# Convolved attention scores from convolved keys and shifted unconvolved values, with the values projected pixel-major for all heads and kept in DRAM

## The chip, the cores and the metric

The kernel runs on one core of a Trainium2 chip. The metric is the device time of one execution in microseconds, as the median of several executions. All data are 32-bit floats. The engines are named as the profile names them: PE (matrix multiply; PEld are its weight loads), DVE (vector), ACT (scalar), POOL (GpSimd) and SP, which here only issues transfers (DMAs).

## The reference

Two layers are applied to a batch of 4 images with 512 channels and 64 × 64 pixels. Layer 0 is a linear attention over two sets of 64 heads; layer 1 is a set of edge filters. The change lies in layer 0.

```
q, k, v = h @ wq.T, h @ wk.T, h @ wv.T                    # 1x1 projections, 512 -> 512 each
qkv = concat([q, k, v])                                   # 1536 channels = 64 heads x (8 q, 8 k, 8 v)
dw  = conv5x5_depthwise(qkv)                              # SAME padding, one 5x5 kernel per channel
pw  = conv1x1_grouped(dw)                                 # groups of 8 channels
f   = concat([qkv, pw]).reshape(B, 128 heads, 24, 4096)   # 64 plain heads, 64 convolved heads
query, key, value = relu(f[:, :, :8]), relu(f[:, :, 8:16]), f[:, :, 16:]
value_pad = concat([value, ones])                         # 9 rows
scores = einsum('bhdn,bhen->bhde', value_pad, key)        # 9 x 8 per head, summed over the 4096 pixels
out = einsum('bhde,bhen->bhdn', scores, query)
out = out[:, :, :8] / (out[:, :, 8:] + 1e-15)
y = conv1x1(out, proj_kernel) * inv + shift + x           # 1024 -> 512 channels
# layer 1: Sobel, Laplace, diagonal and gradient maps of y, four 512 -> 128 branches with GELU,
# an attention over channels, a 512 -> 512 fuse, a norm over channels, GELU, + y
```

For a convolved head the score of value row d and key row e is a sum over pixels of (convolved value d) × (convolved key e). The convolution of the value is linear: it is a weighted sum over 25 shifts and 8 channels of the plain value.

## The kernel before

**Layout.** The heads are cut into four groups of 16 (`Group`, `g` = 0 to 3), so one group has 128 channels each of keys, values and queries, one channel per partition. An image is cut into eight strips of 512 pixels: `STRIPS` names them by half (rows 0 to 31, 32 to 63) and by `k`; strip `k` holds the rows `k`, `k + 4`, ... of its half. There are 16 groups of work in all (4 images × 4).

**A group's work.** `project` (L199) multiplies a strip of x by a 128-column weight matrix (four matmuls of 128 × 512 into one PSUM bank), ACT copies it to `strip`, and four DMAs write it into `inps[t]`, a padded image in the layout that the convolution needs. `turn` (L232) transposes keys and values to pixel-major tiles on PE, and `scores` (L245) forms the plain scores from them. `convolve` (L318) does the 5 × 5 and 1 × 1 convolution of one half of the image for keys, values or queries: 10 shifts × 16 matmuls on 32 × 32 tiles of the PE array, with weights `mat` that POOL builds. `conv_turn` (L349) transposes convolved keys and values, `conv_scores` (L361) makes their scores: each matmul gives 32 × 32 products, of which only the 8 × 8 blocks of equal heads are kept, by a mask in `conv_sums` (L378). `conv_fold` (L406) multiplies the convolved scores into the projection, `conv_denominators` and `conv_divide` (L417, L426) make the convolved heads, and `denominators` and `divide` the plain ones. Results go to DRAM (`heads`, `cheads`, `folded`).

**The order of the work.** PE's instructions stand in the order in which the program writes them; the order on the other engines and on SP is made by the framework from priorities and buffers. `keys_and_values` writes out the first part of a group (16 projections, seven `turn`, six `scores`, with the query convolution of the group before between them), `queries` the second (eight projections, the last `turn` and two `scores`, four convolutions of keys and values, their turns and scores). After each step `run` calls `advance`, which lets a share of the later stages of the image before run on PE: `project_out` (the 1024 → 512 projection), `edge_branches` (filters and branches) and `fuse_out`. The share is in proportion to a cost that is written beside each step (`T_PROJ` = 3.4, `T_CONV` = 8.6 and so on). So image 0 has no other stage beside it, images 1 to 3 have the later stages of the image before between their steps, and the later stages of image 3 stand alone at the end.

**Buffers.** x strips pass through `xst` (five tiles of 128 × 1024), weights through `gw`, most intermediate tiles through `work` (22 tiles of 128 × 512). All DMAs are issued by SP, on one queue, in order. In PSUM four banks hold single tiles (`ps_tile`) and four hold the quads of `convolve` and of the divisions (`quad_tiles`).

Of the kernel before, what the change touches and what calls it, by code (L numbers as in the profile page):

```python
# [15 lines left out]
P = 128  # L16
# [21 lines left out]

NB = H // 4 + 1
STRIPS = [(half, k) for half in range(2) for k in range(4)]  # L40
DXS = (0, -2, -1, 1, 2)

# [3 lines left out]
for _name, _n in (("ident", P), ("bdmask", P), ("hmask", 32), ("spread", P), ("csum", P), ("mmask", 4), ("jmask", 4)):  # L46
    CONST[_name] = slice(_at, _at + _n)
    _at += _n
# [8 lines left out]
T_PROJ, T_TURN, T_SCORES, T_CONV, T_SMALL = 3.4, 0.9, 0.3, 8.6, 0.9  # L57
# [8 lines left out]
def conv_seq_kernel(  # L66
    ctx: ExitStack, tc, x, wqkv, dpk, proj, projc, bn0, consts, vec, watt1, batt1, watt2, wbr, wfuse, out
# [11 lines left out]
    gw = front.enter_context(tc.tile_pool(name="gw", bufs=3))  # L79
    work = front.enter_context(tc.tile_pool(name="work", bufs=22))  # L80
# [8 lines left out]
    def quad_tiles(name):  # L89
        return [psum.tile([P, 512], F32, tag="quad", name=name) for _ in range(4)]  # L90

# [24 lines left out]
    for t in (KEY, VALUE, QUERY):  # L116
        inps[t] = keep.tile([P, 4, NB, W], F32, name=f"inp{t}")
        nc.gpsimd.memset(inps[t][:, :, 0, :], 0.0)
        nc.gpsimd.memset(inps[t][:, :, NB - 1, :], 0.0)

    vts = []
    for n in range(3):
        vt = keep.tile([P, 4, 4, 33], F32, name=f"vt{n}")
        nc.gpsimd.memset(vt, 1.0)
        vts.append(vt)

# [47 lines left out]
    class Group:  # L174


        def __init__(self, b, heads, cheads, folded, g):
            self.b, self.heads, self.cheads, self.folded, self.g = b, heads, cheads, folded, g
            self.w, self.mat, self.xs = {}, {}, {}
            self.strip, self.rq, self.held, self.conv = {}, {}, {}, {}  # L180
# [3 lines left out]
        def load_w(self, t):  # L184
            self.w[t] = gw.tile([P, NCH, P], F32, name="w_sb", tag="w_sb")
            nc.sync.dma_start(out=self.w[t], in_=wqkv[self.g, t])

        def load_mat(self, t):

            dp = gw.tile([P, 4, 48], F32, name="dp_sb", tag="dp_sb", bufs=2)  # L190
            nc.sync.dma_start(out=dp, in_=dpk[self.g, t])
# [15 lines left out]
        def project(self, t, j):  # L207
            half, k = STRIPS[j]
            if t != VALUE and j not in self.xs:
                self.load_x(j)  # L210
            ps = ps_tile("proj")
# [4 lines left out]
            if t != KEY:  # L216
                del self.xs[j]
            s = work_tile("strip")
            nc.scalar.copy(s, ps)  # L219
            self.strip[t, j] = s  # L220
# [4 lines left out]
            if t == QUERY:  # L225
                rq = work_tile("rq")
                nc.gpsimd.tensor_scalar(rq, self.strip.pop((t, j)), 0.0, None, ALU.max)  # L227
                self.rq[j] = rq
# [4 lines left out]
        def turn(self, j):  # L233
            kt_ps, vt_ps = ps_tile("tr"), ps_tile("tr")
            for n in range(4):
                nc.tensor.transpose(kt_ps[:, ts(n, P)], self.strip[KEY, j][:, ts(n, P)], ident)
            kt = work_tile("kt")
            nc.scalar.activation(kt, kt_ps, AF.Relu)
            for n in range(4):
                nc.tensor.transpose(vt_ps[:, ts(n, P)], self.strip[VALUE, j][:, ts(n, P)], ident)  # L240
            vt = vts[j % 3]
            nc.vector.tensor_copy(
                vt.rearrange("p n q d -> p (n q) d")[:, :, 0:32], vt_ps.rearrange("p (a d) -> p a d", d=32)
            )
            self.held[j] = kt, vt  # L245
            del self.strip[KEY, j], self.strip[VALUE, j]

        def scores(self, j):
            kt, vt = self.held.pop(j)
            ps = ps_tile("s")  # L250
            for n in range(4):
                for q in range(4):
                    nc.tensor.matmul(  # L253
                        ps[32 * q : 32 * q + 32, 0:33], lhsT=kt[:, P * n + 32 * q : P * n + 32 * q + 32],
                        rhs=vt[:, n, q, :], start=(n == 0), stop=(n == 3),
                    )
            if j == 0:
                self.s = small.tile([P, 33], F32, name="s_sb")
# [3 lines left out]
            if j == NJ - 1:  # L262
                self.ks = small.tile([P, 32], F32, name="ks_sb")
                nc.vector.tensor_scalar(self.ks, hmask, self.s[:, 32:33], None, ALU.mult)
                self.sb = small.tile([P, 4, 32], F32, name="sbd", bufs=1)
# [5 lines left out]
        def fold_turn(self):  # L271
# [3 lines left out]
            self.st = small.tile([P, P], F32, name="stt", bufs=1)  # L275
# [44 lines left out]
        def convolve(self, t, half):  # L320
# [14 lines left out]
            for i in range(4):  # L335
                o = work_tile("co")
                if t == KEY:
                    if half == 0 and i == 0:
                        self.ksum = small.tile([P, 2, 4], F32, name="ksum")
                    nc.scalar.activation(o, banks[i], AF.Relu, accum_out=self.ksum[:, half, i : i + 1])  # L340
# [558 lines left out]
```

## Time and profile before

| quantity | value |
|---|---|
| median of 3 runs | 5212.99 us (5206.63 to 5223.82) |
| the profiled execution's own time | 5216.06 us |
| its span in the profile | 5214.3 us |
| image 0, no later stage beside it | 0 to about 800 us |
| images 1 to 3 with the later stages of the image before | about 800 to 4433 us |
| the later stages of image 3 | 4433 to 5214 us |

In the profile a group line gives the source line, the engine, the operation, output <- input, the shapes and the count, then the busy time in us, the mean ns of one, and the idle time of the engine before it with what ended it. A 32-bit matmul is recorded as two passes, so 1,536 projections' matmuls are 3,072 records. Matmuls are pipelined: what a block of them takes is read from the distance of the starts in the timeline, not from the duration of one.

### The profile page before, as it was taken

Reading aid. Unit: us, or ns where it says so; the run is one execution under the profiler, and the core shown is the slowest. Engines: PE = TensorE matmul, PEld = TensorE weight load, DVE = VectorE, ACT = ScalarE, POOL = GpSimd, SP = SyncE. Lnnn points to the kernel's source line nnn. Section 1 sums busy time; section 2 is a strip of 40 time slices with the busy share of each in tenths; the row PEclk is TensorE's granted clock in tenths of the full one; section 3 lists DMA queues with packets and bytes.
Section 4 is the critical chain, followed back from the end, with each engine's and each line's share of the span. In section 5 each row is a group of like instructions: output and inputs, shape, how many; then the busy total and the mean of one; then the engine's idle time right before and its main releaser. Section 6 shows DMA issues by size and latency. Waiting matters only on the chain. (4 is left out here: it accounts for less than half of the span.)

```text
span 5214.3 us, 116246 instructions
## 1 busy us (share of the span) xinstructions
PE 4864.4 (93%) x50514; PEld 2567.1 (49%) x50514; DVE 2185.7 (42%) x3084; ACT 1616.6 (31%) x2569; POOL 638.1 (12%) x435
## 2 busy tenths in 40 slices
PE   8999999998999999999999999999989999899777
PEld 3544444444555554444455555444445555445443
DVE  1222222113555643421355645342124655446975
ACT  1111111001444533300134443331013544225765
POOL 1010110000101012300010000240000101000335
PEclk9999999999999999999999999999999999899989
DMA  5445455664544544576545454657654544575435
GB/s 180 145 159 158 150 180 174 154 149 120 174 153 154 172 152 158 182 203 151 151 143 175 138 176 140 187 171 205 149 144 151 182 143 150 151 185 143 147 116 167
DMA packets 534095, 832.18 MB, mean 160 GB/s; under 512 B 192464, under 2 KB 264656, under 8 KB 531536
## 3 DMA queue, kind: packets, MB, share of 16 engines
q1 hardware_dynamic: 533584, 824.74, 53.7%
q8 instruction: 397, 6.50, 0.5%
q14 instruction: 114, 0.93, 0.1%
HBM read 546.09 MB, written 177.75 MB: 139 GB/s over the span
## 5 line engine op out<-in xcount | busy, mean ns | idle before, releaser
L213 PE MATMUL proj<-xt,w_sb 128*128 128x512 f32 x3072 | 1426.2, 609 | 85.7 <-DMA xt<-in_x 51.9
L328 PE MATMUL cv<-inp,mat 32*32 32x504 f32 (+2 forms) x30720 | 1061.9, 594 | 25.6 <-issue 20.3
L213 PEld LDWEIGHTS proj<-xt,w_sb 128*128 128x128 f32 x3072 | 572.2, 194 | 778.2 <-issue 640.0
L528 PE MATMUL yps<-hd,fold_sb 128*128 128x512 f32 x2048 | 897.2, 595 | 15.5 <-DMA hd<-heads 15.4
L328 PEld LDWEIGHTS cv<-inp,mat 32*32 32x32 f32 x30720 | 627.0, 103 | 440.8 <-issue 214.7
L528 PEld LDWEIGHTS yps<-hd,fold_sb 128*128 128x128 f32 x2048 | 386.5, 190 | 508.2 <-issue 475.7
L219 ACT COPY strip<-proj 128x512 f32<-128x512 f32 x384 | 223.6, 583 | 1299.8 <-PE proj L213 1263.4
L603 PE MATMUL br<-maps,wbr_sb 128*128 128x256 f32 x2048 | 484.1, 389 | 40.5 <-ACT maps L586 25.3
L533 DVE SCALAR_TENSOR_TENSOR yt<-yps,shift,xr 128x512 f32<-128x512 f32 x128 | 96.0, 750 | 935.9 <-PE yps L528 880.0
L681 PE MATMUL zps<-ef,wf_sb 128*128 128x512 f32 x1024 | 461.5, 602 | 18.4 <-DVE z L685 8.7
L603 PEld LDWEIGHTS br<-maps,wbr_sb 128*128 128x128 f32 x2048 | 392.1, 194 | 161.8 <-issue 58.9
L227 POOL TENSOR_SCALAR rq<-strip 128x512 f32<-128x512 f32 x128 | 213.2, 1666 | 1789.9 <-ACT strip L219 1167.2
L193 POOL TENSOR_TENSOR mat<-dp_sb 128x1280 f32<-128x1280 f32 x48 | 117.7, 2453 | 1786.6 <-PE cv L328 1136.9
L681 PEld LDWEIGHTS zps<-ef,wf_sb 128*128 128x128 f32 x1024 | 195.8, 193 | 264.4 <-issue 233.0
L576 DVE TENSOR_TENSOR maps<-dv 128x1054 f32<-128x1054 f32 x128 | 164.0, 1281 | 349.4 <-PE br L603 349.4
L610 ACT ACTIVATE ef_o<-br,shift,scale 128x256 f32<-128x256 f32 x256 | 142.4, 560 | 374.1 <-PE br L603 362.3
L292 DVE RECIPROCAL rec<-rec 128x512 f32<-128x512 f32 x64 | 214.4, 3351 | 1.6
L688 POOL TENSOR_TENSOR total<-total,sq 128x512 f32<-128x512 f32 x96 | 129.8, 1352 | 681.2 <-ACT sq L683 667.3
L685 DVE TENSOR_SCALAR z<-zps,fbias 128x512 f32<-128x512 f32 x128 | 95.0, 744 | 260.2 <-DMA out<-z 90.0
L706 POOL TENSOR_TENSOR z<-z,yr 128x512 f32<-128x512 f32 x128 | 174.3, 1379 | 227.4 <-ACT z L703 125.0
L582 ACT ACTIVATE lap<-maps 128x524 f32<-128x524 f32 x128 | 81.6, 638 | 315.8 <-DVE maps L580 311.5
L261 DVE TENSOR_TENSOR s_sb<-s_sb,s 128x33 f32<-128x33 f32 x112 | 20.8, 186 | 370.2 <-PE s L253 370.2
(121 smaller groups left out, 4131.0 us busy)
## 6 DMA issues: line engine op xcount, KB each, us to landing
xt<-in_x SPq DMA_DIRECT2D x512, 512.0 KB, 4.9
inp<-strip SPq DMA_DIRECT2D x1536, 64.0 KB, 2.7
win<-y SPq DMA_DIRECT2D x128, 396.0 KB, 4.3
y<-yt SPq DMA_DIRECT2D x128, 264.0 KB, 4.8
yr<-y SPq DMA_DIRECT2D x128, 264.0 KB, 3.4
xr<-in_x SPq DMA_DIRECT2D x128, 256.0 KB, 5.8
heads<-q SPq DMA_DIRECT2D x128, 256.0 KB, 3.1
hd<-heads SPq DMA_DIRECT2D x128, 256.0 KB, 6.6
```

The costliest lines, as they stand in the source:

```text
L213: nc.tensor.matmul(ps, lhsT=self.w[t][:, c, :], rhs=self.xs[j][c], start=(c == 0), stop=(c == NCH - 1))
L219: nc.scalar.copy(s, ps)
L227: nc.gpsimd.tensor_scalar(rq, self.strip.pop((t, j)), 0.0, None, ALU.max)
L292: nc.vector.reciprocal(rec, rec)
L328: nc.tensor.matmul(rows(banks[i])[32 * j : 32 * j + 32, :, c0:c1], lhsT=self.mat[t][q, j, (dx + 2) * 8 + 4 * b : (dx + 2) * 8 + 4 * b + 4, :],
L528: nc.tensor.matmul(ps, lhsT=fold_sb[g // NG][:, g % NG, ts(c, P)], rhs=hd[g], start=(g == 0), stop=(g == 2 * NG - 1),)
L576: nc.vector.tensor_sub(flat[:, half : 3 * half - 2], dvs[:, 2 : 2 * half], dvs[:, 0 : 2 * half - 2])
L603: nc.tensor.matmul(rows(ps)[:, 4 * n : 4 * n + 4, :], lhsT=wbr_sb[:, k, c, :], rhs=rows(maps[c // 2][:, slot[k], c % 2, :], WB)[:, :, 0:W] ...
L610: nc.scalar.activation(o[:, n, :], ps[:, 256 * n : 256 * n + 256], AF.Gelu, bias=shift1[:, k : k + 1], scale=scale1[:, k : k + 1], accum_o ...
L681: nc.tensor.matmul(ps, lhsT=wf_sb[:, k, ts(c, P)], rhs=ef[k], start=(k == 0), stop=(k == 3))
L688: nc.gpsimd.tensor_add(total, total, sq)
L706: nc.gpsimd.tensor_add(rows(z), rows(z), rows(yr, WB)[:, :, 1 : W + 1])
```

## The change

Convolved values are no longer formed. The score of a convolved head is written as a sum over the 25 shifts of (weight) × (product of the convolved key with the shifted plain value), and the 1 × 1 part of the value convolution is folded into the output projection.

- **Values.** In the first group of an image, after each key projection, `values` projects the values of all 512 channels for 128 pixels at a time: the x strip is the stationary operand, the 512 columns of `wv` move. DVE copies the PSUM bank into one of three tiles with a column of ones beside each 32 values, and three DMAs write it to two DRAM tensors: `turned` (for the plain scores, loaded again per group and strip by `load_turned`) and `near` (padded by two pixels, with the layout head block, block of four rows, column, row, value).
- **Correlation.** `conv_scores` and the value half of `conv_turn` and `turn` go. `correlate` multiplies convolved keys (128 pixels stationary, 32 columns) with 5 × 4 shifted rows of 8 values (160 columns): 16 matmuls for each of 16 steps a group. `weigh` multiplies two PSUM banks with a table of the 5 × 5 weights (`wtab`) and sums them on DVE.
- **Loads for it.** `load_near` loads tiles of 128 × 1320 floats from `near`: 20 a group, through a pool `vals` of four tiles. Four are asked for at the end of `keys`, the others one by one as `correlate` steps release tiles.
- **The rest of the fold.** `mix` forms projection × 1 × 1 kernel once per group of image 0 and keeps it in DRAM; `conv_heads` spreads the scores; `conv_fold` is one full matmul instead of four narrow ones.
- **Pixel order.** Within a strip the rows are interleaved, so that 128 pixels are two rows that lie 16 apart; the ACT copies undo this for `inps`, and `project_out` stores y in two DMAs instead of one.
- **Others.** The relu of a query strip moves from POOL (from `strip`) to ACT (from PSUM); the relu of a key strip is a DVE operation from PSUM. `divide(1)` moves into the next group's first steps. The pools become `work` 18, `gw` 2, `vals` 4, and the written costs of the steps change.

```diff
-T_PROJ, T_TURN, T_SCORES, T_CONV, T_SMALL = 3.4, 0.9, 0.3, 8.6, 0.9
+T_PROJ, T_TURN, T_SCORES, T_CONV, T_CORR, T_SMALL = 3.4, 0.5, 0.3, 10.6, 1.1, 0.9
+
+
+WORK, VALS = 18, 4
...
-    gw = front.enter_context(tc.tile_pool(name="gw", bufs=3))
-    work = front.enter_context(tc.tile_pool(name="work", bufs=22))
+    mini = front.enter_context(tc.tile_pool(name="mini", bufs=2))
+    gw = front.enter_context(tc.tile_pool(name="gw", bufs=2))
+    vals = front.enter_context(tc.tile_pool(name="vals", bufs=VALS))
+    work = front.enter_context(tc.tile_pool(name="work", bufs=WORK))
...
+    near = [dram.tile([2 * NG, NB, W + 4, 4, 66], F32, name=f"near{n}", bufs=1) for n in range(2)]
+    turned = [dram.tile([NG, NJ, P, 4, 132], F32, name=f"turned{n}", bufs=1) for n in range(2)]
...
+            self.nears = iter([(half, jp, b) for half in range(2) for jp in range(2) for b in range(5)])
...
+        def values(self, j, c):
+
+            half, k = STRIPS[j]
+            ps = ps_tile("val")
+            for n in range(NCH):
+                nc.tensor.matmul(
+                    ps, lhsT=self.xs[j][n][:, ts(c, P)], rhs=self.wv[n], start=(n == 0), stop=(n == NCH - 1)
+                )
+            vt = vts[c % 3]
+            nc.vector.tensor_copy(vt[:, :, 0:32], ps.rearrange("p (a d) -> p a d", d=32))
+            if c == 3:
+                del self.xs[j]
+            flat = vt.rearrange("p a d -> p (a d)")
+            nc.sync.dma_start(
+                out=turned[self.b % 2][:, j, :, c, :].rearrange("g p d -> p g d"),
+                in_=flat.rearrange("p (g d) -> p g d", g=NG),
+            )
+            b = 8 * half + c + (k + 2) // 4
+            for a in range(2):
+                nc.sync.dma_start(
+                    out=near[self.b % 2][:, b + 4 * a, 2 : W + 2, (k + 2) % 4, :].rearrange("a x d -> x a d"),
+                    in_=flat[64 * a : 64 * a + 64].rearrange("p (a d) -> p a d", d=66),
+                )
+
+        def load_turned(self, j):
+            self.vt[j] = gw.tile([P, 4, 132], F32, name="vt_sb", tag="vt_sb", bufs=3)
+            nc.sync.dma_start(out=self.vt[j], in_=turned[self.b % 2][self.g, j])
...
-            kt_ps, vt_ps = ps_tile("tr"), ps_tile("tr")
-            for n in range(4):
-                nc.tensor.transpose(kt_ps[:, ts(n, P)], self.strip[KEY, j][:, ts(n, P)], ident)
-            kt = work_tile("kt")
-            nc.scalar.activation(kt, kt_ps, AF.Relu)
-            for n in range(4):
-                nc.tensor.transpose(vt_ps[:, ts(n, P)], self.strip[VALUE, j][:, ts(n, P)], ident)
-            vt = vts[j % 3]
-            nc.vector.tensor_copy(
-                vt.rearrange("p n q d -> p (n q) d")[:, :, 0:32], vt_ps.rearrange("p (a d) -> p a d", d=32)
-            )
-            self.held[j] = kt, vt
-            del self.strip[KEY, j], self.strip[VALUE, j]
...
+            if not self.g:
+                self.load_turned(j)
+            kt_ps = ps_tile("tr")
+            for c in range(4):
+                nc.tensor.transpose(kt_ps[:, ts(c, P)], self.strip[j][:, ts(c, P)], ident)
+            self.held[j] = work_tile("kt")
+            nc.scalar.copy(self.held[j], kt_ps)
+            del self.strip[j]
...
+        def load_near(self, count):
+
+            for _ in range(count):
+                half, jp, b = at = next(self.nears, (None,) * 3)
+                if half is not None:
+                    self.near[at] = vals.tile([P, 5 * VROW], F32, name="near", tag="vals")
+                    v = near[self.b % 2][2 * self.g + jp, 8 * half + b]
+                    block, column = (W + 4) * VROW, VROW
+                    nc.sync.dma_start(
+                        out=self.near[at],
+                        in_=bass.AP(v.tensor, v.offset, [[4 * block, 2], [column, W], [1, 5 * VROW]]),
...
+        def correlate(self, half, jp, c):
+
+            if c == 0:
+                self.banks = [psum.tile([P, 512], F32, tag="quad", name="corr") for _ in range(2)]
+            for n in range(2):
+                for b in range(2):
+                    v = self.near[half, jp, c + b].rearrange("p (x r d) -> p x r d", r=4, d=66)
+                    for i in range(4):
+                        at = P * c + 32 * (2 * jp + n)
+                        nc.tensor.matmul(
+                            self.banks[n][32 * i : 32 * i + 32, 160 * b : 160 * b + 160],
+                            lhsT=self.held["c", i][:, at : at + 32],
+                            rhs=v[:, :, :, 33 * n + 8 * i : 33 * n + 8 * i + 8],
+                            start=(c == 0 and b == 0), stop=(c == 3 and b == 1),
+                        )
+            if c == 3:
+                self.weigh(half, jp)
+            del self.near[half, jp, c]
+            if c == 3:
+                del self.near[half, jp, 4]
+            self.load_near(2 if c == 3 else 1)
...
+        def weigh(self, half, jp):
+
+            if half == 0 and jp == 0:
+                self.ct = mini.tile([P, 2, 4, 8], F32, name="ct", bufs=1)
+            for n in range(2):
+                w = work_tile("weighed", 320)
+                nc.vector.tensor_mul(w, self.banks[n][:, 0:320], self.wtab[:, 2 * jp + n, :])
+                nc.vector.tensor_reduce(
+                    self.ct[:, half, 2 * jp + n, :], w.rearrange("p (a d) -> p d a", d=8), AX.X, ALU.add
+                )
...
+            ps = ps_tile("heads_ps")
+            nc.tensor.matmul(
+                ps[:, 0:8], lhsT=self.cst.rearrange("p i j d -> p (i j d)"), rhs=table["esel"], start=True, stop=True
+            )
...
+            return sum([
+                pj(0), q("divide", 1), q("conv_sums"), pj(1), q("mix"), q("conv_heads"), q("convolve", QUERY, 0), tr(0),
+                pj(2), q("conv_fold"), q("conv_denominators", 0), sc(0), tr(1), pj(3), q("conv_divide", 0), sc(1), tr(2),
+                pj(4), q("convolve", QUERY, 1), sc(2), tr(3), pj(5), q("conv_denominators", 1), sc(3), tr(4), pj(6),
+                q("conv_divide", 1), sc(4), tr(5), [(0.0, self.load_wtab)], pj(7), [(0.0, lambda: self.load_near(VALS))],
+                sc(5), tr(6),
+            ], [])
...
+                pj(0), own("scores", 6), own("turn", 7), pj(1), cv(0), pj(2), own("scores", 7), ct(0, 0), ct(0, 1), pj(3),
+                ct(0, 2), ct(0, 3), own("denominators", 0), own("fold_turn"), pj(4), own("divide", 0), pj(5), co(0, 0),
+                pj(6), co(0, 1), own("fold"), cv(1), pj(7), ct(1, 0), ct(1, 1), own("denominators", 1), ct(1, 2), ct(1, 3),
+                co(1, 0), co(1, 1),
...
-                    nc.sync.dma_start(out=y[c, :, at : at + 29 : 4, :], in_=yt)
+                    for a in range(2):
+                        nc.sync.dma_start(out=y[c, :, at + 16 * a : at + 16 * a + 13 : 4, :], in_=yt[:, a::2, :])
...
```

## The prediction

> **What bounds the kernel now.** First the page, its parts 1 to 3:
>
> ```profile
> PE 4864.4 (93%) x50514; PEld 2567.1 (49%) x50514; DVE 2185.7 (42%) x3084; ACT 1616.6 (31%) x2569; POOL 638.1 (12%) x435
> PEclk9999999999999999999999999999999999899989
> DMA  5445455664544544576545454657654544575435
> q1 hardware_dynamic: 533584, 824.74, 53.7%
> ```
>
> PE is busy 93% at nearly full clock; DVE, ACT and POOL have room, and so has the DMA, as long as a transfer is spread over all 16 engines. So PE's work sets the time, and what leaves PE shortens the kernel. The stages follow from the windows, with images 0 (one group, then two) and 1 to 3:
>
> ```profile
> 199.50:399.80 200.30, 192.19 (x2833) 99.25 (x2830) 48.37 (x76) 32.79 (x65) 19.07 (x11) 0.97 0.49 154
> 800.00:4430.00 3630.00, 3463.03 (x37390) 1835.00 (x37390) 1496.21 (x2169) 1091.90 (x1774) 392.91 (x250) 0.98 0.55 161
> ```
>
> Columns: length, then busy time of PE, PEld, DVE, ACT, POOL, then clock, DMA share, GB/s. A group lasts 200 us in image 0, where PE idles 8, and 302.5 us (3630 / 12) in images 1 to 3. Third, PE's timeline of one group gives the price of each step:
>
> ```profile
> 376.30 11.06 PE L328 MATMUL cv<-inp,mat 32*32 32x512 f32 x320
> 392.83 1.06 PE L353 MATMUL ctr<-consts_sb,co 128*128 128x128 f32 x4
> 397.03 0.46 PE L368 MATMUL cs<-ckt,cvt 128*32 128x32 f32 x32
> 2529.09 0.66 PE L236 MATMUL tr<-consts_sb,strip 128*128 128x128 f32 x4
> 2529.58 0.60 PE L240 MATMUL tr<-consts_sb,strip 128*128 128x128 f32 x4
> 2530.01 3.60 PE L213 MATMUL proj<-xt,w_sb 128*128 128x512 f32 x8
> 2547.28 1.07 PE L421 MATMUL cden<-co,kc_sb 128*32 128x512 f32 x8
> 2548.28 3.70 PE L213 MATMUL proj<-xt,w_sb 128*128 128x512 f32 x8
> ```
>
> From start to start: four transposes 0.43 to 0.5 us, four column-tiled matmuls of 512 columns 1.0 us, a projection 3.5. Last, DMA sizes and landings (page part 6):
>
> ```profile
> xt<-in_x SPq DMA_DIRECT2D x512, 512.0 KB, 4.9
> hd<-cheads SPq DMA_DIRECT2D x128, 256.0 KB, 7.1
> ```
>
> Half a megabyte lands in 4.9 us while others run.
>
> **The change on PE.** Per group it removes two value convolutions (11.06 us each, 1061.9 / 96), eight value transposes in `turn` (0.43), eight in `conv_turn` (0.45) and eight `conv_scores` (0.39): 22.1 + 3.4 + 3.6 + 3.1 = 32.2 us. The value projections keep their count and size (32 per image of 128 pixels × 512 values, in place of 32 of 128 values × 512 pixels). It adds 16 `correlate` steps of 16 column-tiled matmuls with 160 columns. Two rows bound a step: scaling the 512-column set of `cden` (4 sets × 1.0 × 160 / 512 = 1.24 us), and the line through it and the 33-column `scores` (0.39 for 4 sets), 1.34 us. No row has a moving operand in runs of 8 elements; were they twice as slow a step would cost 2.7. I take 1.34: 21.4 us. `conv_heads` less the narrower `conv_fold` is about 0.2. Net −10.6 us a group, −170 in all. In image 0 some waits go as well (PE on POOL's rq 1.3, the division behind DVE's copies 2.2, transposes at 0.85 instead of 0.45 while they wait for copies, 3.4): −28 in four groups.
>
> **Other engines.** DVE loses three PSUM copies a strip and gains the key relu, the `values` copy (both like `vt`, 688 ns) and `weigh`, 128 products and 128 sums of 320 elements under 0.7 us each; ACT takes rq from POOL (0.58 us × 128). All lie under PE; without that cover they would be 200 us. The DMA loses 512 stores of 64 KB and the larger `projc` loads. It gains 256 stores in 264-byte packets and 128 in 528-byte ones (the trace's packet records have 264-byte packets at a median of 19 ns, so one value step holds each engine about 2 us in its 3.5), 128 loads of `turned`, 128 further y stores. In the built order of SP, the next x strips stand behind the value stores, so about every second strip of an image's first group waits some 4 us: +16 for image 0, half elsewhere, about +40. In number SP gets 412 more transfers (4,109 for 3,697) of 0.4 to 0.6 us of issue, 200 us spread over a queue with room. Every load of `near` makes SP wait for the `correlate` step that frees its tile; behind it in the built order stand an x half-strip, the four inp stores of a query strip and the heads stores, and each transfer also waits for the eighth before it to land. With quick loads that costs nothing, since PE has those strips already; with slow ones it is the delay counted below.
>
> **The loads of `near`: the place that decides.** 320 loads of 676 KB, 128 rows of 5,280 bytes. In the packet records 4,096 bytes take a median of 159 ns and 8,192 take 309, so 5,280 take about 202. Spread over 16 engines that is 8 packets each, 1.6 us, and landings near xt's 4.9. But every SP transfer of the kernel before has an outermost dimension of 128, 64, 32 or 16; this one's source is written as 2 × 64 × 1320, and the built program carries it so against a destination of 128 × 1 × 1320. [...] No row of the trace shows a transfer on two engines. By the row a load costs 1.6 us of engine time; by the rule 64 packets × 202 ns = 12.9 us on each of two engines, through which every other transfer's share also passes. By the row the forecast is faster, by the rule slower. [...]
>
> **What two engines make of a group.** `vals` holds four tiles. They are filled ahead of the first `correlate`; the other 16 loads can start only as its steps release tiles, so they fall between the first and the last step of the group. That stretch is two times two `correlate`, two query projections, one key convolution, four turns: 16 × 1.34 + 7 + 11 + 4 + 2 = 45 us of PE. The 16 loads take 16 × 12.9 = 207. Walking through it: the first is asked for at 1.3 us and starts at about 3; then they follow each other until the four tiles of the second half are in, at 133; the projection in front of the second half waits for an x half-strip that SP issues behind these loads; the next request leaves at 142, and the last step ends at about 223. In image 0 that is 223 instead of 45, and two of the next group's four loads delay its projc and x strips by some 20: a group takes 145 (the rest, 190 − 45) + 223 + 20 = 388, against 200, four times: +750.
>
> In images 1 to 3 the stretch holds 70 us of PE with the later stages between. Their DMA work takes the two engines too: 0.55 × 302 = 166 us a group, about 125 at the undisturbed packet times, so 33 in a stretch of 23% of the written costs. win, hd and xr loads queue behind up to three loads of `near` (39 us) and PE meets them in written order: I add 20 us for the times when this leaves the two engines without a request, and 15 in the rest of the group (between 0 and 70 together). PE without the stretch is 302.5 − 15 − 70 = 217 (15 of savings here, since a third of the saved waits is in image 0 alone). So 217 + 15 + 223 + 33 + 20 = 508 against 302.5: +205, twelve times, +2460. The PE savings are inside both sums. 5216 + 750 + 2460 = 8430 on the profiled execution's scale, 3 us above the median. Without the 35 for late stage loads it is 8000; with these loads passing in the gaps of PE's waits 7600; with 70, 8850. I say 8250, between the first two, since some late stage loads will fall into waits that are counted already.
>
> **Rivals.** (1) The loads are spread over 16 engines, whatever the outermost dimension. For it: the xt and hd rows[...]. Then PE's sum counts: −170 − 28 + 40, and waits for `near` remain, since step 4 of each `correlate` needs a tile asked for two steps earlier (2.7 us against a landing of 4 to 5), and 676 KB per 1.34 us is over what the engines move: 7 us a group in image 0, 3 with other stages between, +64. 5216 − 170 − 28 + 40 + 64 = 5122, call it 5120; with the array-time price of a step and fewer waits 4990. It decides if the landing of a load is below about 5 us; two to three times that is where the gain is used up. (2) 16 engines, but the short runs of `correlate`'s moving operand halve its rate: +340 on rival 1, about 5460, slower. Against it: `br` with runs of 64 elements streams at the rate of unbroken rows. (3) The change doesn't relieve PE as written: PE's order does contain no value convolution, so only the price can be off, not the fact.
>
> **How the numbers follow.** Two engines 0.86, rival 1 0.10, rival 2 and the like 0.04. The range 7300 to 9300 takes in the bounds above (7600 to 8850) and the uncertain packet time under load, and holds about 0.94 of the first case, 0.81 in all. Chances against 0.3% (15 us, about what the spread of the runs before lets one tell): faster 0.10, within 0.01, slower 0.89.
>
> **What would show it.** Right: near<-near lands in 13 us and more, up to 50 when queued; PE's longest waits are at `correlate` for DMA near; the stretch from first to last step is over 200 us; PE is busy under 65%; the clock sags in those stretches; the DMA share falls although more bytes move. Wrong: landings of 4 to 6 us and PE still over 90%: then rival 1. A `correlate` step of 2.5 us without a wait: rival 2. A time of 6000 to 7000 would say that more than two engines, or more than four tiles' worth of overlap, serve the loads.

## The result, and the profile after

The changed kernel takes 8484.22 us (median; 8464.37 to 8494.72) against 5215.22 us before: 1.626 times as long, 95% interval 1.622 to 1.631. The prediction said 8250 us, 7300 to 9300. Runs on other chips are compared below by their ratio to the kernel before on the same chip; "at 5216" is such a ratio times 5216 us.

The page of the profiled execution, parts 1 to 3 and the row of `correlate`:

```profile
span 8462.6 us, 101898 instructions
...
PE 5026.1 (59%) x43290; PEld 2589.3 (31%) x43290; DVE 2219.4 (26%) x3088; ACT 1595.2 (19%) x2569; POOL 392.2 (5%) x291
...
PEclk8676757688786858699778676779779767777998
DMA  7332424364362525367444243436445343424644
...
q1 hardware_dynamic: 769760, 1110.97, 43.7%
...
L450 PE MATMUL corr<-near,ckt 128*32 128x160 f32 x8192 | 509.1, 404 | 2145.7 <-DMA near<-near 2071.9
```

PE fell from 93% busy to 59%, though it has 7,224 instructions fewer. The row at the bottom names the reason: PE stood for 2071.9 us in front of `correlate`. The queue line looks harmless and is not: it moved 1111 MB instead of 825 and yet was busy for a smaller share, 43.7% instead of 53.7%. The packets took more time (on average over the engines 3698 us, 43.7% of 8463, instead of 2800, 53.7% of 5214), but the span grew still more: in a stretch where two engines of 16 work, the share is only an eighth.

PE's waits, first of the whole execution, then of the first group alone (time in all, times, longest):

```profile
PE corr L450 <- DMA near<-near: 2071.9, 191, 22.9
PE proj L262 <- DMA xt<-in_x: 652.0, 44, 55.5
PE yps L647 <- DMA hd<-heads: 174.1, 16, 36.4
PE mix L493 <- DMA projc<-in_projc: 85.0, 4, 24.9
```

```profile
PE corr L450 <- DMA near<-near: 133.0, 12, 14.4
PE proj L262 <- DMA xt<-in_x: 124.7, 7, 39.7
```

And PE's timeline of one stretch from the first to the last `correlate` of a group in image 0 (start, length, engine, line; in brackets the idle time before):

```profile
662.09 4.01 PE L450 MATMUL corr<-near,ckt 128*32 128x160 f32 x104
680.54 1.83 PE L450 MATMUL corr<-near,ckt 128*32 128x160 f32 x24 [14.43 <-DMA near<-near]
...
706.39 2.36 PE L450 MATMUL corr<-near,ckt 128*32 128x160 f32 x32 [12.10 <-DMA near<-near]
...
803.91 3.78 PE L262 MATMUL proj<-xt,w_sb 128*128 128x512 f32 x4 [39.80 <-DMA xt<-in_x]
...
854.11 2.36 PE L450 MATMUL corr<-near,ckt 128*32 128x160 f32 x32 [11.92 <-DMA near<-near]
867.00 2.36 PE L450 MATMUL corr<-near,ckt 128*32 128x160 f32 x32 [10.53 <-DMA near<-near]
879.95 2.36 PE L450 MATMUL corr<-near,ckt 128*32 128x160 f32 x32 [10.59 <-DMA near<-near]
892.66 1.83 PE L450 MATMUL corr<-near,ckt 128*32 128x160 f32 x24 [10.35 <-DMA near<-near]
...
928.91 2.07 PE L493 MATMUL mix<-projc,pwb 128*128 128x512 f32 x2 [23.93 <-DMA projc<-in_projc]
```

Read the start times, not the lengths. From 854.11 to 879.95 a step begins every 12.9 us: PE takes each tile when it lands, and a tile lands every 12.9 us. The stretch lasts from 662.09 to 894.49 = 232 us (892.66 + 1.83), where its PE work alone was estimated at 45 us. At 803.91 and 928.91 one sees what queues behind the near loads: an x half-strip and the next group's `projc`.

Two windows, with the columns length, busy time of PE, PEld, DVE, ACT, POOL, granted clock as a share of full speed, DMA share, GB/s. The first ends with the last work before the first pause, the second is the row of single steps at the end of the stretch:

```profile
642.45:666.10 23.65, 23.17 (x206) 11.86 (x201) 7.15 (x9) 9.02 (x21) 0.00 (x0) 1.00 0.65 207
820.00:890.00 70.00, 9.67 (x128) 5.21 (x128) 2.34 (x4) 0.00 (x0) 0.00 (x0) 0.50 0.13 53
```

In the second the DMA share is 0.13, and two of 16 are 0.125. PE's clock is half of full speed there, and some 2 us of work in every 12.9 do not bring it back.

The records of single packets count the engines. They give each packet's size, start and duration; 5,280 bytes is a row of `near` and nothing else. In this execution 5,280-byte packets are under way during 4285 us, and in 4058 of these exactly two at once. The semaphore by which a DMA reports its end says the same: each of the 512 x loads raises it 16 times, each of the 320 `near` loads, with two packets at once, 3 times. Below, DMAs of 62 and of 2 rows raise it 3 times, of 57 rows 4 times, of 7 rows 8 times, and those of 32, 64 and 128 rows 16 times.

### The profile page after: what moved, and what is told of

Its sections match the earlier page's. It is cut to its first block, busy times and chain, and to the rows that moved or that the text cites. A ratio compares the mean times of both kernels' runs of the same rounds, so it can differ in the third digit from the quotient of the medians.

```text
span 8462.6 us, 101898 instructions
## 1 busy us (share of the span) xinstructions
PE 5026.1 (59%) x43290; PEld 2589.3 (31%) x43290; DVE 2219.4 (26%) x3088; ACT 1595.2 (19%) x2569; POOL 392.2 (5%) x291
## 3 DMA queue, kind: packets, MB, share of 16 engines
q1 hardware_dynamic: 769760, 1110.97, 43.7%
## 5 line engine op out<-in xcount | busy, mean ns | idle before, releaser
L450 PE MATMUL corr<-near,ckt 128*32 128x160 f32 x8192 | 509.1, 404 | 2145.7 <-DMA near<-near 2071.9
L262 PE MATMUL proj<-xt,w_sb 128*128 128x512 f32 x2048 | 1063.2, 664 | 694.5 <-DMA xt<-in_x 652.0
L450 PEld LDWEIGHTS corr<-near,ckt 128*32 128x32 f32 x8192 | 305.6, 140 | 2352.3 <-DMA near<-near 2093.6
L262 PEld LDWEIGHTS proj<-xt,w_sb 128*128 128x128 f32 x2048 | 412.3, 213 | 1186.0 <-issue 615.0
L401 PE MATMUL cv<-inp,mat 32*32 32x512 f32 (+1 forms) x20480 | 708.8, 600 | 18.0 <-issue 16.3
L401 PEld LDWEIGHTS cv<-inp,mat 32*32 32x32 f32 x20480 | 417.3, 104 | 306.3 <-issue 142.3
L285 PE MATMUL val<-wv_sb,xt 128*128 128x512 f32 x1024 | 456.8, 599 | 0.3 <-DVE vt L289 0.3
L285 PEld LDWEIGHTS val<-wv_sb,xt 128*128 128x128 f32 x1024 | 197.4, 193 | 247.8 <-issue 243.5
L413 ACT ACTIVATE co<-cv 128x512 f32<-128x512 f32 x128 | 74.4, 595 | 971.9 <-PE cv L401 971.9
L689 DVE TENSOR_TENSOR dv<-win 128x528 f32<-128x528 f32 x128 | 92.2, 721 | 494.8 <-DMA win<-y 493.9
```

The costliest lines, as they stand in the source:

```text
L262: nc.tensor.matmul(ps, lhsT=self.w[t][:, c, :], rhs=self.xs[j][c], start=(c == 0), stop=(c == NCH - 1))
L285: nc.tensor.matmul(ps, lhsT=self.xs[j][n][:, ts(c, P)], rhs=self.wv[n], start=(n == 0), stop=(n == NCH - 1))
L401: nc.tensor.matmul(rows(banks[i])[32 * j : 32 * j + 32, :, c0:c1], lhsT=self.mat[t][q, j, (dx + 2) * 8 + 4 * b : (dx + 2) * 8 + 4 * b + 4, :],
L450: nc.tensor.matmul(self.banks[n][32 * i : 32 * i + 32, 160 * b : 160 * b + 160], lhsT=self.held["c", i][:, at : at + 32], rhs=v[:, :, :, 3 ...
L689: nc.vector.tensor_sub(down, below, above)
```

## The experiments

Each time the near loads are the only thing changed, unless it is said otherwise. The theory on trial first: **(T)** the load is cut for two engines, because its source is written with an outermost 2. Against it: that what costs is the three-level source pattern, or that 676 KB (660.0 in the profile, which counts 1,024 bytes as a KB) are too much even for 16 engines.

**1. The same rows with 64 as the outermost dimension.**

```
-  dma(out=near_tile,                  in_=[[4*block, 2], [column, 64], [1, 1320]])
+  for a in 0, 1:
+      dma(out=near_tile[64a : 64a+64], in_=offset 4*block*a, [[column, 64], [1, 1320]])
```

> Each tile of near is loaded by two transfers of 64 rows with a source of 64 x 1320 (both outermost dimensions 64), in place of one of 128 rows with a source of 2 x 64 x 1320; the same bytes to the same places, nothing else changed. Two-engine theory: the rows are now spread over 16 engines, a tile costs 8 packets per engine (1.6 us) and the time falls to that of rival 1 of the prediction, about 5120 us (4990 to 5230); DMA near waits of PE fall from 2072 us to under 150, PE is busy over 90%. Rival theory (the bytes of near themselves, 216 MB more, or the latency of a load asked for only when a tile is free): the bytes and the order are the same, so the time stays above 7500 us.

Measured: 5635.46 us, ratio 1.0795 [1.0775, 1.0814]. Of the 3269 us that the change cost, 2850 go with this one edit. But at 5635 us instead of the expected 4990 to 5230 it is not faster than before, as rival 1 of the prediction would have had it. Page, part 1, 3, 5 and 6 (the last column is the landing time in us):

```profile
PE 4835.3 (86%) x43290; PEld 2518.9 (45%) x43290; DVE 2226.7 (39%) x3088; ACT 1598.8 (28%) x2571; POOL 399.5 (7%) x291
...
q1 hardware_dynamic: 779360, 1111.00, 72.4%
...
L451 PE MATMUL corr<-near,ckt 128*32 128x160 f32 x8192 | 404.8, 345 | 266.8 <-DMA near<-near 259.4
...
near<-near SPq DMA_DIRECT2D x640, 330.0 KB, 7.2
```

`correlate` waits 259 us instead of 2072, and the queue's share is 72.4%, with the same megabytes in more engines. Something is still slow: half a tile lands in 7.2 us, more than a whole 512-KB x load (5.6 in this run).

**2 to 4. Two engines, three and seven, and sixteen, with the same simple source.** The two-level source stays; only the cut of the 64 rows differs.

```
   for a in 0, 1:
+      for first, last in (0, 62), (62, 64):      # second kernel: (0, 57), (57, 64); third: (0, 32), (32, 64)
           dma(out=near_tile[64a+first : 64a+last], in_=[[column, last-first], [1, 1320]])
```

> Each tile of near is loaded by four transfers with plain two-dimensional patterns, of 62 + 2 + 62 + 2 rows. The largest divisor up to 16 of 62 and of 2 is 2. Two-engine theory: again 64 packets on each of two engines, 12.9 us a tile, so about 8480 us as in the changed kernel (8200 to 8800), although no pattern has three dimensions any more. Rival (the three-dimensional pattern of the source is what is slow): about 5100 to 5250 us.

> Four transfers a tile, of 57 + 7 + 57 + 7 rows; the largest divisors up to 16 are 3 and 7. Two-engine theory (engines = that divisor[...]): the busiest engines get 2 x (19 + 1) = 40 packets, 8.1 us a tile, so 16 tiles take 129 us in place of 207, 78 us less in each of 16 groups: 8480 - 1250 = about 7230 us (6900 to 7500). Rival (uneven cuts are slow as such, or any transfer on few engines costs the same): as the 62-row cut, about 8480; or, if the number of engines doesn't matter, about 5150.

> Four transfers a tile, of 32 rows each: divisor 16. It controls for the number of transfers in the two cut kernels. Two-engine theory: about the time of the two transfers of 64 rows, plus at most 100 us for 640 more issues on SP (0.4 to 0.6 us each, partly on the path): 5120 to 5250 us. Rival (four transfers a tile are what makes the cut kernels slow): over 7000 us.

Measured, one execution each: 8556, 7027 and 5641 us. The rows of `correlate` (62 + 2 rows; then 57 + 7), and the wait of the third:

```profile
L455 PE MATMUL corr<-near,ckt 128*32 128x160 f32 x8192 | 506.1, 402 | 2029.1 <-DMA near<-near 1967.3
```

```profile
L455 PE MATMUL corr<-near,ckt 128*32 128x160 f32 x8192 | 484.5, 389 | 1098.3 <-DMA near<-near 1076.9
```

```profile
PE corr L455 <- DMA near<-near: 256.9, 117, 7.8
```

62 = 2 × 31 brings the whole loss back with a plain source pattern (8556 us), so the pattern's third level is not the cause. 57 = 3 × 19, with 7 beside it, lies between (7027 us). The packets under way show it directly: two at once for 4048 of 4368 us with 62 rows, three for 2254 of 2813 us with 57 + 7, sixteen as the commonest count with 64 and with 32. For 7 rows the semaphore speaks alone: 8 rises, where two packets at once gave 3 and three gave 4, from which seven are inferred. Experiment 4 has twice the DMAs of experiment 1 and the same time, so the number of DMAs is not the cause either. As far as these cuts go, the number at once is the largest one up to 16 that divides the outermost dimension of the source: two for 2 × 64, for 62 and for 2 rows, three for 57, seven for 7, sixteen for 32 and 64. Others were not tried. Which engines serve is not shown: the packet records do not name them. The 19 + 1 packets on one engine in the expectation for 57 + 7 rows are its author's estimate.

**5 and 6. Why 16 engines were not enough: which rows of SBUF are written.** The packets gave the clue. A 5,280-byte packet has a median of 202 ns in the kernel with the change and 362 ns in experiment 1; in experiment 4, 361. Packets of 4,096 bytes stay at 159 in all of them. Two theories: (A) What costs is which rows of SBUF a DMA of half a tile writes, 0 to 63 or 64 to 127, a conjecture of the author's that no run before had shown. (B) Sixteen engines hinder each other in DRAM, because the rows that they read overlap (5,280 bytes every 1,056). To part them, pixels are renumbered: a chunk's pixel (row a, column x) goes to partition 2x + a instead of 64a + x. Experiment 5 loads 128 rows in one DMA, 6 loads them in two whose source is that of experiment 1 to the letter, and whose destination is every second row.

```
   x in DRAM, the key strips and the convolved keys: pixels in the order 2x + a within a chunk
   (the last sum with x reads a second copy of x in the old order)
-  near store of values:  in_=flat[64a : 64a+64]
+  near store of values:  in_=flat[a::2]
   experiment 5:  dma(out=near_tile,       in_=[[column, 64], [4*block, 2], [1, 1320]])
   experiment 6:  dma(out=near_tile[a::2], in_=offset 4*block*a, [[column, 64], [1, 1320]])   # a = 0, 1
```

> The pixels of a chunk are put in the order 2x + a instead of 64a + x (a: which of the two rows), so that one DMA with the columns outermost, [[column, 64], [4 block, 2], [1, 1320]], fills all 128 rows of a near tile and is cut for 16 engines; the two value stores of a chunk read every second row. Same arithmetic. Theory A[...]: the 5,280-B packets fall from 359 ns in the 64-row version back to about 205 ns, the tile lands in 4 to 5 us instead of 7.2, the queue's share falls from 72% by 6 to 7 points, the wait of correlate for near from 259 us to under 100; time 5300 to 5480. Theory B (16 engines reading overlapping rows of one 72-KB block hinder each other in DRAM): packets stay near 350 ns, time 5600 to 5680.

> As the kernel with the order 2x + a, but each near tile by two DMAs of 64 rows, one for each a, whose destination is every second row of the tile; the source of each DMA is letter for letter that of the first 64-row version (5635 us, packets 359 ns). Theory A[...]: the packets are at about 205 ns, as with one DMA of 128 rows, time within 1.5% of that kernel. Theory B (source): packets near 350 ns, time about 5635.

Measured: 5469.48 us, ratio 1.0441 [1.0416, 1.0466], and 5524.36 (two executions), ratio 1.0550 [1.0521, 1.0579].

| near load | 5,280-B packet, median (mean) ns | PE waits for near, us | ratio to before |
|---|---|---|---|
| rows 0–63 and 64–127, two DMAs (exp. 1) | 362 (359) | 259.4 | 1.0795 |
| four DMAs of 32 rows (exp. 4) | 361 (352) | 256.9 | 1.081 (one execution) |
| every second row, two DMAs (exp. 6) | 202 (254) | 175.9 | 1.0550 |
| all 128 rows, one DMA (exp. 5) | 202 (245) | 154.6 | 1.0441 |

Same source, other rows of SBUF, and the median falls from 362 to 202 ns. So B falls and A is borne out: it matters which rows are written. A DMA of rows 0 to 63 (362 ns) does no better than one of 32 rows (361). Why these rows are slow the records don't show. An estimate, as if sixteen packets were always under way: 16 × 5,280 B / 362 ns = 233 GB/s for the half, 16 × 5,280 B / 202 ns = 418 GB/s for all rows.

Not all went as expected. In experiment 5 the mean packet was expected at 205 ns and takes 245, a tenth of the packets take 301 and more, and why is not shown; the wait for near was expected under 100 us and is 154.6; the queue's share was to fall by 6 to 7 points and fell from 72.4 to 71.0%. By the ratios, which were taken on two chips, writing every second row is worth 2.4 points (1.0795 to 1.0550, the renumbering's other edits included) and one DMA in place of two another 1.1. The remaining 4.4% needs another explanation.

**7 and 8. Does SP's order delay the x strips?** Beside near, PE waits most for x. In an image's first group each x strip is requested behind 12 value stores, of which each waits for its copy.

```
   in project(KEY, j), first group of an image:
+      self.load_x(j + 1)            # ahead of the value stores of strip j
```

> The order 2x + a, and in the first group of an image the x strip after the one that is projected is requested before the value stores of this one, not behind them. If the start of an image is late because the x loads stand behind 12 value stores in SP's queue, the wait of proj for xt falls from about 150 us to under 80, the first group of images 1 to 3 gets 10 to 25 us shorter each, and the time falls 50 to 110 us below the kernel with the order alone. If the DMA engines are what is short there (264,192 packets of 264 B at 23 ns), the wait stays within 30 us of the former and so does the time.

> The 64-row version (two DMAs of 64 rows per near tile, 5635 us) with the x strip requested one ahead in the first group. If SP's order is what delays x: 5540 to 5590. If the DMA engines are short: within 20 us of 5635. The wait of correlate for near (259 us) should stay in both.

Measured: with the order 2x + a 5442.24 us, ratio 1.0398 [1.0381, 1.0414]; with 64-row halves 5654.03 us, ratio 1.0797 [1.0781, 1.0813], no change. PE's waits of the first, then of the second:

```profile
PE corr L455 <- DMA near<-near: 160.0, 78, 7.6
PE proj L267 <- DMA xt<-in_x: 120.8, 24, 31.1
```

```profile
PE corr L453 <- DMA near<-near: 258.3, 121, 8.9
PE proj L264 <- DMA xt<-in_x: 139.1, 23, 35.0
```

The wait for x falls by 45 us (165.9 in experiment 5) and by 13 (152.3 in experiment 1), the time by 0.4% and by nothing. The first groups of images 1 to 3 (469, 554 and 546 us, after 473, 546 and 544) did not get shorter; only image 0's did, from 338 to 318. So SP's order costs some 20 us at the very beginning, and the theory is wrong for the rest.

**9. Without most of the near traffic.** Of each five tiles the first alone is loaded, and all steps multiply it.

```
   load_near, from experiment 5:
+      if b > 0: the tile is that of b = 0, no DMA
```

> Order 2x + a, one DMA per tile (5469 us), but only the first of each five near tiles is loaded (64 loads instead of 320); the other four steps multiply that same tile again, so the conv heads' scores are those of another sum. PE's instructions stay. It takes 173 MB and 8,2 ms of packet time (5,280 B at 245 ns) away: 0.5 ms of each DMA engine. Theory A (what is left of the loss is the near traffic, by its own waits of 155 us, by PE's clock of 0.938 against 0.969, and by what x and hd loads wait behind it): 5150 to 5250, the wait of correlate under 30 us, the clock at 0.96 or more, the wait of proj for xt under 120 us. Theory B (the rest is the start of each image, where the value stores are): only the 155 us and some clock go: 5280 to 5330, the wait for xt stays near 165, first groups of images 1 to 3 within 10 us of 473, 546, 544.

Measured: 5126.47 us, ratio 0.9824 [0.9803, 0.9846]: 5124 at 5216, 5.9% under experiment 5. PE's busy time and the row of `correlate`, then a group of image 0 in this kernel and in the one before (columns as in the windows above):

```profile
PE 4691.9 (92%) x43290; PEld 2484.9 (49%) x43290; DVE 2216.4 (43%) x3088; ACT 1597.0 (31%) x2569; POOL 392.1 (8%) x291
...
L455 PE MATMUL corr<-near,ckt 128*32 128x160 f32 x8192 | 326.7, 310 | 7.3 <-ACT ckt L428 6.9
```

```profile
300.00:462.00 162.00, 148.77 (x2318) 81.55 (x2318) 46.79 (x71) 31.75 (x66) 4.79 (x2) 0.97 0.63 205
```

```profile
203.00:403.00 200.00, 191.90 (x2830) 99.19 (x2829) 48.37 (x76) 32.79 (x65) 19.07 (x11) 0.97 0.49 154
```

PE has the changed kernel's work here and hardly its loads, and that work is indeed smaller: 148.8 us in a group instead of 191.9 at the same clock. Of these 43 us some 28 are the eight value projections that moved to the image's first group (8 × 3.5); the rest is what the change saves. A `correlate` step is busy for 326.7 / 256 = 1.28 us. So theory A of this experiment stands, and the time is even below its 5150: what experiment 5 lost lies in the loads of near and in what they delay. It is the only version faster than the kernel before, and it leaves out four fifths of the loads.

**10. Without half of the near stores.** The near stores of images 2 and 3 are left out, on top of experiment 5; `correlate` reads those of images 0 and 1 again.

> Order 2x + a, one DMA per tile (5469 us), but the values of images 2 and 3 are not stored in the near layout (their conv heads read those of images 0 and 1): half of the 264-B near stores, some 131,000 packets at 26 ns, 3.4 ms or 0.21 ms of each engine, are gone. If the small stores are what makes the start of an image long: the first groups of images 2 and 3 fall by 30 to 60 us each (from 546 and 544), image 1's (473) stays, time 5370 to 5410. If not: each within 12 us, time 5440 to 5470.

Measured: 5389.31 us, ratio 1.0325 [1.0303, 1.0347], 1.1% under experiment 5, some 60 us at 5216. The time is where the theory of the stores had it, the place is not: the first groups of images 2 and 3 fell by 19 us each (546 to 527, 544 to 525), not by 30 to 60, and those of images 0 and 1, whose stores are all there, by 11 and 16 (338 to 327, 473 to 457). The expectation also counted twice the packets: the records have 198,656 packets of 264 bytes here and 264,192 in experiment 5, so 65,536 are gone and not 131,000. Half of the near stores cost about 1%; where is not shown.

**11 and 12. More tiles ahead.** A step needs tiles c and c + 1, so with four tiles two loads are ahead of PE. The twelfth kernel also issues the loads for `mix` at the end of the group before.

```
-  WORK, VALS = 18, 4
+  WORK, VALS = 15, 5                # experiment 11, on top of 7
+  WORK, VALS = 13, 6                # experiment 12, with load_mix() moved behind co(1, 1)
```

> The order 2x + a with the x strip one ahead (5442 us), with five near tiles instead of four and 15 instead of 18 work tiles. A step needs two tiles, so four leave two loads ahead of PE, five leave three. If latency is what correlate waits on: its wait falls from 160 us to under 100 and the time to 5370 to 5420. If the engines' throughput in the stretch is: the wait stays over 130, time 5420 to 5480.

> As the kernel with five near tiles (5277 us), with six near tiles and 13 work tiles, and the loads of projc, pw and pc issued at the end of the group before, not in front of the product that needs them. If correlate still waits on how far ahead its loads are: its wait falls from 78 us to 30 to 50, with the clock and PE's work worth 40 to 60 us in all; the wait of mix for projc (31.5 us) goes: 5180 to 5230, level with the kernel before (5214) or just under it. If the near loads are short of throughput by now: the wait stays over 65 us, time 5230 to 5260. If 13 work tiles are too few: PE's other waits grow and the time is over 5280.

Measured: five tiles 5277.11 us, ratio 1.0112 [1.0090, 1.0134], below the expected 5370 to 5420; six 5254.51 us, ratio 1.0041 [1.0027, 1.0055]. PE's waits with five, then with six:

```profile
PE proj L267 <- DMA xt<-in_x: 110.3, 24, 28.2
PE corr L455 <- DMA near<-near: 78.0, 64, 3.5
```

```profile
PE proj L267 <- DMA xt<-in_x: 128.9, 24, 32.8
PE cv L406 <- issue: 67.0, 49, 4.0
PE corr L455 <- DMA near<-near: 45.9, 55, 2.5
```

With four, five and six tiles `correlate` waits 160, 78 and 46 us, so what was left was a lack of requests ahead rather than of throughput. The fifth tile brings 2.8% (1.0398 to 1.0112), with three work tiles fewer. Six tiles end 0.4% above the kernel before, 5237 at 5216 where 5180 to 5230 was expected: the wait for near fell as expected, but that for x rose by 19 us, and PE's gaps without a visible releaser (67.0; 61.2 with five) stayed. No version with all its loads is faster than the kernel before.

## Why the prediction was right, and where it was not

**Two engines, 12.9 us a tile: right, and shown.** The spacing in the timeline is 12.9 us, the packets take 202 ns (mean 211), two are under way at a time, and in the kernels with 62 and 57 rows two and three. Here the prediction set a row of the trace, 16 engines, against what it calls the rule: two engines for a source of 2 × 64 × 1320, an assumption of its author that no row of the kernel before showed. It built its sum on the assumption, and that held.

**The walk through a group: right within a few per cent.** The stretch was said to be 223 us and is 232. The x half-strip and `projc` wait behind the loads as written (39.80 and 23.93 us; "some 20" was said of the second). The mean group of images 1 to 3 lasts 500 us (6005 / 12) where 508 was said, that of image 0 418 (1672 / 4) where 388 was said.

**The sum by images.** Image 0 cost +872 (1672 us instead of 800), the other three +2372, the end +5. Predicted were +750 and +2460; the 16 us that the prediction names for x in image 0 are not in its sum. So image 0 was put 122 us too low. Its four stretches account for 36 of these (9 each). Some 61 are the start: in the first group PE waits 124.7 us for x, of which 39.7 are the half-strip of the stretch; that leaves 85, against 24.3 before. The last 25 were not traced. Images 1 to 3 were put 88 us too high, of which some 50 are a slip: 23% of 125 us are 29 and not 33, twelve times. A word on reading the groups: the first lasts 525 us and the others 375, 373 and 398, and most of that difference is no wait. All 32 value projections of the image now stand in the first group (at 3.5 us 112), which the prediction's even count leaves out and the sum of an image doesn't show.

**The last choice was the wrong one.** The sum was 8430, the measured span 8463. That it came so near is in part luck, since the 122 us and the 88 us go against each other. The prediction then went down to 8250 because some late stage loads would fall into waits already counted. The group of 500 us lies beside the 508 of the full sum, so little of it can have fallen there.

**Rival 1 was mis-sized.** Its PE term is sound: in experiment 9, where the loads are nearly gone, PE is busy for 4691.9 us instead of 4864.4, 172 less where 170 was said, and a `correlate` step takes 1.28 us where 1.34 was said. That this kernel's 5124 (at 5216) meets rival 1's 5120 is luck: it has none of the 64 us of waits for near that stand in that sum, but longer waits elsewhere (x 116.6 us instead of 51.9, where 40 more were allowed for, and 27.8 for `projc`). The price of the loads was wrong. It had +64 us of waits for near; the 64-row version has 259. Four things were missing. Rows 0 to 63 or 64 to 127 alone, with sixteen engines at work, make a packet 362 instead of 202 ns, 2.4 points of the time. Four tiles are too few (a half tile lands in 7.2 us, a step takes 1.28), 2.8% for one tile more. Other transfers are waited for: x 152 us instead of 51.9, hd (the heads, loaded for the late stages) 46.2 instead of 15.4. And PE's clock falls with its pauses: 0.927 on average instead of 0.969 (0.778 in the kernel with the change), so that the remaining work takes longer (PE is busy for 4835.3 us, in experiment 9 for 4691.9). Rival 1's threshold, that the gain is used up at two to three times a landing of 5 us, is wrong for the same reason: at 7.2 us the kernel is 8% slower. PE's waits before, then in experiment 1:

```profile
PE proj L213 <- DMA xt<-in_x: 51.9, 11, 8.4
PE yps L528 <- DMA hd<-heads: 15.4, 1, 15.4
```

```profile
PE proj L262 <- DMA xt<-in_x: 152.3, 26, 19.4
PE yps L648 <- DMA hd<-heads: 46.2, 6, 13.7
```

**Rival 2 fell.** In experiment 9 a step takes 1.28 us with the same runs of 8 elements, so they are no burden. (The prediction's `br`, with runs of 64, starts a matmul of 256 columns every 216 ns in the kernel before, and `proj`, with unbroken rows, one of 512 every 429.) In the timeline above a step takes 1.23 us before the first pause (104 records, 32 a step, in 4.01 us) and 2.36 after each pause: that is nearly the 2.7 of this rival, and it comes from the clock, 1.00 in the first window above and 0.50 in the second.

**The marks.** PE under 65% (59%), stretch over 200 us, sagging clock, a lower DMA share with more bytes: all came. That a tile lands in 13 us and more is seen only in the spacing, since the page gives no landing times for these loads.

## What to carry to other kernels

Before a large DMA is trusted with 16 engines, factor the outermost dimension of its source as the built program carries it, and count its packets under way: 2 × 64 and 62 rows had two at once here, 57 rows three, 32 and 64 rows sixteen. A 2 in front made a tile land every 12.9 us (64 packets of 202 ns on each of two engines), where 8 packets on each of 16 would be 1.6 us by estimate; the queue's share over 16 engines did not show it (43.7%), but a wait that repeats at a fixed spacing did. For loads like these, put 128 rows into one transfer (1.0441 of the time before), or, where it has to be halves, let a half be every second partition (1.0550) and not the lower 64 (1.0795). And when matrix work is traded for traffic, price the traffic's own side effects: how many loads can be asked for ahead, whose loads stand behind them, and what PE's pauses do to its clock (0.969 before, 0.778 with the change).

## What the runs showed of the hardware that was not expected

- A 5,280-byte packet has a median of 202 ns when two engines write rows of one half (62 of rows 0 to 63, then 62 of the other, experiment 2), and 362 ns when sixteen do; to every second row sixteen have 202 ns again. With 57 + 7 rows (three and seven engines) the median over both is still 202: one half of the rows was slow with sixteen engines and not in these two runs. Numbers between seven and sixteen were not tried.
- The granted clock is low where PE pauses: 0.70 on average over one group of image 0 with the two-engine loads, 0.97 in one without near traffic. These are the windows of the kernel with the change, one group and then images 1 to 3, with the columns named above:

```profile
901.00:1274.00 373.00, 164.89 (x2319) 85.36 (x2315) 45.06 (x70) 31.57 (x66) 4.80 (x2) 0.70 0.35 118
1672.00:7677.00 6005.00, 3582.42 (x32049) 1845.55 (x32041) 1520.92 (x2175) 1082.10 (x1777) 200.31 (x143) 0.78 0.44 133
```

  A group of image 0 keeps PE busy for 164.89 us here and for 148.77 without near traffic, with the same instructions: the work after a pause gets longer too. In the whole execution PE is busy for 5026.1 us here and for 4691.9 there, with 43290 matmul records each.
- Gaps of PE inside the key and query convolutions without a visible releaser ("issue") mostly grew with the queue's share: 20.3 us before (53.7%), 36.5 in experiment 9 (64.2%), 79.7 in experiment 1 (72.4%). But experiment 4 has 47.6 at 72.0%, so the share alone does not decide. What fills them was not tried.
